# Keys by token in the last stage: a transposing DMA of 16-bit halves in place of TensorE transposes

## The chip, the cores and the metric

The kernel runs on one core of a Trainium2 chip. The core has five engines that each take their own instructions in the order in which the program was built: TensorE (PE in the profile, with its weight loads shown apart as PEld), VectorE (DVE), ScalarE (ACT), GpSimd (POOL) and SyncE (SP, which here only issues DMAs). They meet through semaphores, through SBUF (the on-chip memory), and through PSUM, eight banks of 128 partitions by 512 float32 in which matmuls leave their results. The metric is the device time of one execution in microseconds; the time of a kernel is the median of several runs. One more execution is profiled.

## The reference

The input is x, 8 sequences of 512 tokens with 512 features, float32. The output is x + s * silu(f). Both s and f come from the layer-normed tokens: s is linear attention over each sequence, f a mixture of 16 experts, of which each token takes 4, plus a gated shared expert. The part that the change touches is the attention, with 16 heads of 32 features, in 4 chunks of 128 tokens:

```python
q = (x @ Wq).reshape(b, n, HEADS, HEAD_DIM)
k = (x @ Wk).reshape(b, n, HEADS, HEAD_DIM)
v = (x @ Wv).reshape(b, n, HEADS, HEAD_DIM)
q = _lrpe_rotate(jax.nn.silu(q))
k = _lrpe_rotate(jax.nn.silu(k))
def step(S, qkv):
    qi, ki, vi = qkv
    scores = jnp.einsum('bthd,bshd->bhts', qi, ki) * D[None]
    o_intra = jnp.einsum('bhts,bshd->bthd', scores, vi)
    o_inter = jnp.einsum('bthd,bhde->bthe', qi * decay_q[None, :, :, None], S)
    S_new = lam_C[None, :, None, None] * S + jnp.einsum('bshd,bshe->bhde', ki * decay_k[None, :, :, None], vi)
    return (S_new, o_intra + o_inter)
```

(The two silus are written inside the rotation here; the reference has them on lines of their own.) The result o is gated, normalised by head and multiplied by Wo. The keys are thus needed in two layouts: features on partitions for the scores (qi with ki), and tokens on partitions for the state (ki, decayed, with vi). The state after the last of the four chunks is never used, so three chunks, 384 tokens, are enough for the second layout.

## The kernel before, in words

The kernel has three stages. The first (to about 330 us of the profiled execution) normalises all tokens, computes the routing and the shared expert, and attends over sequences 0 and 1. The second (about 330 to 752) runs 138 expert blocks of 128 gathered tokens; it fetches transposed tokens by a DMA that transposes 16-bit halves (L1019, issued on SP), which ScalarE joins into float32 (L1034). The last stage (752 to the end) attends over sequences 2 to 7 and, between these pieces, gathers and adds up each token's four expert results.

In the last stage `enter(FIRST)` starts sequence 2, `sequence(b, ...)` runs over b = 2 to 6 and `last_sequence` over 7. Each works on four groups g of four heads, that is 128 features. For a group `key` and `query` call `rotated` (L598 to L614): eight matmul instructions into a bank (L602), a silu on ScalarE (L607, tiles sk and sq), a shuffle and three products or sums on VectorE (L609 to L613), which leave kT and qT, features on partitions. `by_token` (L622) makes the second layout of the keys: three TensorE transposes (L629) into the bank pk, and a decaying product on VectorE (L632, tile kd). `scores` (L638) has the state matmuls of kd with v (L647) into the last 96 columns of the same bank pk, the score matmuls (L658) into four banks, and on VectorE the states (L661, L663), the decayed queries qd (L668) and the masked scores sc (L674). `output` (L679) multiplies qd by the state (L686) and sc by v (L692) into one bank, po, and gates it (L696). After the four groups come squares and the norm, and `project` (L735) with Wo, which for b < 7 is spread over the groups of the following sequence.

The PSUM banks go by tags: four "a" (scores, norm), one "k" (pk), one "m" (the key projection) and two "d", which the query projection pq, the projection pw and the output po take in turn. A bank is written again only when its last reader is done. Thus po of group 0 takes the bank of pq of group 2, and waits for the silu sq of group 2 on ScalarE; po of group 1 waits likewise for sq of group 3.

In `sequence`, group g's loop turn runs: scores(g), key(g + 2), by_token(g + 1), a projection, query(g + 2), another projection, output(g). So keys and queries are made two groups ahead. Between such steps, generators of the mixture (`mixture`, L1133) and its end (`last`, L1170) place their instructions: gathers (L1146) and additions (L1152, L1155) on GpSimd, sums on VectorE (L1157, L1160), a silu on ScalarE (L1163), the product with the attention (L1174), the addition of x on GpSimd (L1178) and the store on SP (L1179). The order on every engine is fixed when the program is built.

Of the kernel before, what the change touches and what calls it, by code (L numbers as in the profile page):

```python
# [10 lines left out]
F32 = mybir.dt.float32  # L11
# [3 lines left out]
U16 = mybir.dt.uint16  # L15
# [4 lines left out]
P = 128  # L20
# [75 lines left out]
def tile_block(ctx: ExitStack, tc: tile.TileContext, a: dict, out: bass.AP):  # L96
# [107 lines left out]
    @contextmanager  # L204
    def on_pe():

        with tc.issue_after(last_pe[-1]) if last_pe else nullcontext():
            yield
        traced = nc.cur_bb.bb.instructions
        last_pe.append(next(  # L210
            i for i in reversed(traced) if i.engine == mybir.EngineType.PE))
# [337 lines left out]

    between = [lambda: None]  # L550

    kept = []

    def value(b, t):
        if t == 0:
# [60 lines left out]
    def key(b, g):  # L616
        kT_of[g] = rotated(b, g, "k", wk)
# [4 lines left out]
    def by_token(b, g):  # L622

        if not kept:
            kept.append(bank("k", f"pk_{b}_{g}"))
        pk = kept[0]
        with on_pe():
            for c in range(NC - 1):
                nc.tensor.transpose(  # L629
                    pk[:, c * P : (c + 1) * P], kT_of[g][:, c * C : (c + 1) * C], ident)  # L630
        kd = scr[0].tile([P, NC - 1, HG, HD], F32, tag="kd", name=f"kd_{b}_{g}")
        nc.vector.tensor_tensor(  # L632
            kd, pk[:, : (NC - 1) * P].rearrange("p (c h d) -> p c h d", c=NC - 1, d=HD),
            dk[:, g * HG : (g + 1) * HG].unsqueeze(1).unsqueeze(3).to_broadcast(
                [P, NC - 1, HG, HD]), ALU.mult)
        kd_of[g] = pk[:, (NC - 1) * P :], kd

    def scores(b, g):  # L638

        pkv, kd = kd_of.pop(g)
        with on_pe():
            for c in range(NC - 1):
                for j in range(HG):
                    h = g * HG + j
                    nc.tensor.matmul(  # L647
                        pkv[j * HD : (j + 1) * HD, c * HD : (c + 1) * HD], lhsT=kd[:, c, j, :],
                        rhs=v_of[b][:, c, h * HD : (h + 1) * HD], start=True, stop=True)
        kT, qT = kT_of.pop(g), qT_of.pop(g)  # L650
        sc_of[g] = []
        pss = [bank("a", f"ps_{b}_{g}_{j}") for j in range(HG)]
        with on_pe():
            for c in range(NC):
                cs = slice(c * C, (c + 1) * C)
                for j in range(HG):
                    hs = slice(j * HD, (j + 1) * HD)
                    nc.tensor.matmul(  # L658
                        pss[j][:, cs], lhsT=kT[hs, cs], rhs=qT[hs, cs], start=True, stop=True)
        st = scr[0].tile([P, NC - 1, HD], F32, tag="state", name=f"state_{b}_{g}")  # L660
        nc.vector.tensor_copy(st[:, 0], pkv[:, :HD])  # L661
        for c in range(1, NC - 1):
            nc.vector.scalar_tensor_tensor(  # L663
                st[:, c], st[:, c - 1], lamc[:, g : g + 1], pkv[:, c * HD : (c + 1) * HD],
                ALU.mult, ALU.add)
        st_of[g] = st
        qd = scr[0].tile([P, NC - 1, C], F32, tag="qd", name=f"qd_{b}_{g}")
        nc.vector.tensor_tensor(  # L668
            qd, qT[:, C:].rearrange("p (c t) -> p c t", t=C),
            dq[:, g].unsqueeze(1).to_broadcast([P, NC - 1, C]), ALU.mult)  # L670
        qd_of[g] = qd
        for j in range(HG):
            s = scr[0].tile([P, NC, C], F32, tag="sc", name=f"sc_{b}_{g}_{j}", bufs=4)
            nc.vector.tensor_tensor(  # L674
                s, pss[j].rearrange("p (c t) -> p c t", t=C),
                dmask[:, g * HG + j].unsqueeze(1).to_broadcast([P, NC, C]), ALU.mult)
            sc_of[g].append(s)

    def output(b, g):  # L679
        po = bank("d", f"po_{b}_{g}")  # L680
        st, qd, sc = st_of.pop(g), qd_of.pop(g), sc_of.pop(g)
        with on_pe():
            for c in range(1, NC):
                for j in range(HG):
                    hs = slice(j * HD, (j + 1) * HD)
                    nc.tensor.matmul(  # L686
                        po[hs, c * C : (c + 1) * C], lhsT=st[hs, c - 1, :], rhs=qd[hs, c - 1, :],
                        start=(c == 1), stop=False)
            for c in range(NC):
                for j in range(HG):  # L690
                    h = g * HG + j
                    nc.tensor.matmul(  # L692
                        po[j * HD : (j + 1) * HD, c * C : (c + 1) * C],
                        lhsT=v_of[b][:, c, h * HD : (h + 1) * HD],
                        rhs=sc[j][:, c], start=False, stop=(c == NC - 1))
        nc.vector.tensor_tensor(on_of[b][:, g, :], po, on_of[b][:, g, :], ALU.mult)  # L696
# [43 lines left out]
    def enter(b, step=lambda: None):  # L740

        key(b, 0)
        step()
        query(b, 0)
        step()
        key(b, 1)
        step()
        by_token(b, 0)
        query(b, 1)
        step()  # L750

    def sequence(b, step, projected, before=None, defer=False, also=lambda: None):


        n = b + 1

        def project_tiles(q, ts):
            if q is not None:
                for t in ts:
                    projected(q, t, project(q, t))  # L760


        fill = ([0], [1], [2], [3], [], [], [], [])
        for g in range(G):
            scores(b, g)
            step()
            if g + 2 < G:
                key(b, g + 2)
            else:
                value(n, 2 * (g - 2))  # L770
            if g == 0 and b not in on_of:
                gate_3(b)
            if g + 1 < G:
                by_token(b, g + 1)
            project_tiles(before, fill[2 * g])
            step()
            if g + 2 < G:
                query(b, g + 2)
                if g + 3 == G and n not in xT_of:
                    load_xT(n)  # L780
            elif defer:
                (gate_1, gate_2)[g - 2](n)
            if g + 2 == G:
                value(n, 1)
            project_tiles(before, fill[2 * g + 1])
            if fill[2 * g + 1] == [NC - 1]:
                on_of.pop(before, None)
            output(b, g)
            step()
        v_of.pop(b)  # L790
        if n == FIRST:
            gate_1(n)
            squares(b)
            inverse(b)
            value(n, 3)
            normed(b)
            gate_2(n)
            return
        if defer:
            gate_3(n)  # L800
        value(n, 3)
        also()
        squares(b)
        step()
        inverse(b)
        key(n, 0)
        also()
        query(n, 0)
        normed(b)
        also()  # L810
        step()
        key(n, 1)
        by_token(n, 0)
        query(n, 1)
        also()
        if not defer:
            for gate, half in ((gate_1, [0, 1]), (gate_2, [2, 3])):
                gate(n)
                project_tiles(b, half)
                also()  # L820
            on_of.pop(b)
        step()

    def last_sequence(b, step, projected, before):
# [18 lines left out]
        def normed_of(g):  # L843
            rs = rs_of.pop(g)
            pbs = [bank(tag, f"pb_{b}_{g}_{c}")
                   for c, tag in enumerate("mddk" if g + 1 == G else "aaaa")]
            with on_pe():
                for c in range(NC):
                    cq = slice(c * Q, c * Q + H)
                    nc.tensor.matmul(  # L850
                        pbs[c][:, :C], lhsT=wge[cq, g * P : (g + 1) * P], rhs=rs[cq, :],
                        start=True, stop=True)
            for c in range(NC):
                oc = on_of[b][:, g, c * C : (c + 1) * C]
                nc.vector.tensor_tensor(oc, oc, pbs[c][:, :C], ALU.mult)
# [13 lines left out]
        for g in range(G):  # L869
            scores(b, g)  # L870
            step()
            if g + 2 < G:
                key(b, g + 2)
            if g > 1:
                project_before(2 * g - 3)
            if g:
                squares_of(g - 1)
            if g + 1 < G:
                by_token(b, g + 1)
            step()  # L880
            if g + 2 < G:
                query(b, g + 2)
            if g in (1, 2):
                project_before(2 * g - 2)
                normed_of(g - 1)
            output(b, g)
            step()
        kept.clear()
# [397 lines left out]
```

## Time and profile before

The median of 3 runs is 1228.07 us (1228.03 to 1228.19). The profiled execution:

| what | value |
|---|---|
| its own time | 1229.93 us |
| its span | 1228.1 us |
| mean granted TensorE clock | 0.989 |
| PE busy | 1170.0 us, 95% |
| DVE busy | 754.3 us, 61% |
| POOL busy | 441.8 us, 36% |
| ACT busy | 401.5 us, 33% |
| DMA, mean over the span | 177 GB/s |
| L629 transposes, all 96 | 16.2 us, 277 ns each |
| L1034 joins of the second stage, 138 | 105.8 us, 766 ns each |

Busy time is the time in which an engine executes; waiting on semaphores and issuing DMAs is not counted. The matmuls are pipelined, so the mean of one transpose is longer than the room that it takes between others. The span is from the first to the last instruction seen; the own time is the device's time of that same execution. A row of the timeline gives a start, a length, the engine, the line, the operation with its tiles (out<-in) and shapes, and in brackets how long the engine had been idle and what released it.

### The profile page before, as it was taken

What the parts mean: (1) busy time and instruction counts of PE and PEld (TensorE: products, weight loads), DVE (VectorE), ACT (ScalarE), POOL (GpSimd) and SP (SyncE); (2) the same over time, 40 slices, a digit from 0 to 9 for tenths busy, and PEclk for the clock granted to TensorE, in tenths of its full rate; (3) what the DMA queues carried; (4) which work ended last, traced back from release to release, by engine and by line L of the source; (5) the groups of instructions that cost most, each with busy time, mean ns of one, the idle gap of its engine ahead of it and who ended that gap; (6) DMA issues with size and microseconds to landing.
All of it is one profiled execution on the core that took longest, in us unless ns stands there. A gap on an engine that the chain in (4) does not pass through costs nothing. (4 is left out here: it accounts for less than half of the span.)

```text
span 1228.1 us, 21368 instructions
## 1 busy us (share of the span) xinstructions
PE 1170.0 (95%) x7734; PEld 690.8 (56%) x7734; DVE 754.3 (61%) x1638; ACT 401.5 (33%) x767; POOL 441.8 (36%) x426
## 2 busy tenths in 40 slices
PE   6998999989989999999999999999999999999997
PEld 3444554446467777777777775545545444445453
DVE  6378554899324444444444445849879589598784
ACT  3342333320264444444443441041140221411420
POOL 3222101100213333333333332833867827848211
PEclk9998999989999999999999999999999899999999
DMA  9784331182459999999998997822746626535011
GB/s 322 259 289 161 117 137 70 26 323 82 169 142 225 231 229 224 230 228 225 224 228 223 232 225 231 288 61 77 259 112 215 183 67 226 169 104 149 24 36 69
DMA packets 164599, 217.76 MB, mean 177 GB/s; under 512 B 90896, under 2 KB 99856, under 8 KB 162576
## 3 DMA queue, kind: packets, MB, share of 16 engines
q1 hardware_dynamic: 143216, 145.52, 39.9%
q0 software_dynamic: 21280, 70.88, 20.8%
q8 instruction: 64, 1.05, 0.4%
q14 instruction: 39, 0.32, 0.1%
HBM read 125.89 MB, written 72.35 MB: 161 GB/s over the span
## 5 line engine op out<-in xcount | busy, mean ns | idle before, releaser
L1051 PE MATMUL pgu<-wexp,xt 128*128 x1104 | 261.4, 380 | 0.8 <-ACT xt L1032 0.8
L1051 PEld LDWEIGHTS pgu<-wexp,xt 128*128 128x128 f32 x1104 | 209.0, 190 | 88.5 <-issue 42.8
L1010 POOL DMA_INDIRECT xg<-xn_d,slot x80 | 75.9, 949 | 248.5 <-DVE y L1081 162.5
L1056 DVE TENSOR_TENSOR slb<-slb,pgu 128x128 f32<-128x128 f32 x138 | 39.6, 287 | 196.4 <-ACT slb L1055 129.9
L1146 POOL DMA_INDIRECT yg<-y_d,posi x128 | 141.1, 1102 | 46.9 <-SPq L1113 19.3
L1034 ACT COPY xt<-pl 128x512 uint16<-128x512 uint16 x138 | 105.8, 766 | 140.2 <-DMA pl<-xg 86.8
L1072 PE MATMUL py<-wexp,hT 128*128 x276 | 141.3, 594 | 0.1
L560 PE MATMUL pv<-wv,xT 128*128 128x512 f32 x256 | 123.5, 622 | 5.2 <-DVE sh L372 4.1
L602 PE MATMUL pk<-xT,wk 128*128 128x512 f32 x256 | 120.5, 611 | 1.7 <-DVEq L1113 1.7
L602 PE MATMUL pq<-xT,wq 128*128 128x512 f32 x256 | 115.9, 593 | 0.0
L1178 POOL TENSOR_TENSOR xo<-xo,m 128x512 f32<-128x512 f32 x30 | 43.4, 1446 | 167.5 <-DVE m L1174 158.5
L735 PE MATMUL pw<-wo,on 128*128 128x512 f32 x224 | 100.8, 595 | 2.5 <-ACT so L908 1.8
L1010 POOL DMA_INDIRECT more<-xn_d,slot x58 | 54.8, 944 | 111.4 <-DVE y L1081 110.5
L560 PEld LDWEIGHTS pv<-wv,xT 128*128 128x128 f32 x256 | 47.4, 197 | 63.6 <-issue 55.6
L674 DVE TENSOR_TENSOR sc<-ps,dmask 128x512 f32<-128x512 f32 x128 | 79.4, 682 | 1.0 <-PE ps L658 1.0
L1081 DVE TENSOR_SCALAR y<-py,xg 128x512 f32<-128x512 f32 x80 | 60.0, 751 | 29.2 <-PE py L1072 28.8
L602 PEld LDWEIGHTS pq<-xT,wq 128*128 128x128 f32 x256 | 47.3, 191 | 52.2 <-issue 50.9
L602 PEld LDWEIGHTS pk<-xT,wk 128*128 128x128 f32 x256 | 46.4, 192 | 51.1 <-issue 48.6
L735 PEld LDWEIGHTS pw<-wo,on 128*128 128x128 f32 x224 | 41.3, 190 | 52.1 <-issue 44.7
L1055 ACT ACTIVATE slb<-pgu 128x128 f32<-128x128 f32 x138 | 38.3, 278 | 93.3 <-PE pgu L1051 88.9
L607 ACT ACTIVATE sk<-pk 128x512 f32<-128x512 f32 x32 | 19.1, 596 | 124.2 <-PE pk L602 102.4
L564 ACT COPY v<-pv 128x512 f32<-128x512 f32 x32 | 18.8, 588 | 122.2 <-PE pv L560 118.3
(168 smaller groups left out, 1766.7 us busy)
## 6 DMA issues: line engine op xcount, KB each, us to landing
y_d<-y SPq DMA_DIRECT2D x138, 256.0 KB
wexp<-in_experts SPq DMA_DIRECT2D x16, 768.0 KB
sh_d<-sh SPq DMA_DIRECT2D x32, 256.0 KB
m<-sh_d SPq DMA_DIRECT2D x32, 256.0 KB
xo<-in_x SPq DMA_DIRECT2D x32, 256.0 KB
out<-xo SPq DMA_DIRECT2D x32, 256.0 KB
x<-in_x SPq DMA_DIRECT2D x7, 1024.0 KB
xT_d<-xT SPq DMA_DIRECT2D x7, 1024.0 KB
```

The lines of the kernel that those rows point to most:

```text
L560: nc.tensor.matmul(pv, lhsT=xT_of[b][:, k, t * P : (t + 1) * P], rhs=wv[:, k, :], start=(k == 0), stop=(k == KC - 1))
L602: nc.tensor.matmul(ps, lhsT=w[:, k, g * P : (g + 1) * P], rhs=xT_of[b][:, k, :], start=(k == 0), stop=(k == KC - 1))
L674: nc.vector.tensor_tensor(s, pss[j].rearrange("p (c t) -> p c t", t=C), dmask[:, g * HG + j].unsqueeze(1).to_broadcast([P, NC, C]), ALU.mult)
L735: nc.tensor.matmul(pw, lhsT=on_of[b][:, g, t * P : (t + 1) * P], rhs=wo[:, g, :], start=(g == 0), stop=(g == G - 1))
L1010: nc.gpsimd.indirect_dma_start(out=row(i), out_offset=None, in_=xn_d, in_offset=bass.IndirectOffsetOnAxis(ap=slot[:, i : i + 1], axis=0))
L1034: nc.scalar.copy(xt[:, KP:, :].bitcast(U16).rearrange("p k (t h) -> p h k t", h=2), turned(i).rearrange("p (h k) t -> p h k t", h=2))
L1051: nc.tensor.matmul(pg[:, : 2 * F], lhsT=xt[:, k, :], rhs=wflat[:, bass.ds(off + k * 2 * F, 2 * F)], start=(k == 0), stop=(k == KC - 1))
L1056: nc.vector.tensor_tensor(sl, sl, pg[:, F : 2 * F], ALU.mult)
L1072: nc.tensor.matmul(py, lhsT=hT_of.pop(i), rhs=wflat[:, bass.ds(off_of.pop(i) + KC * 2 * F, D)], start=True, stop=True)
L1081: gone.append(nc.vector.tensor_scalar(y, py, row(i).bitcast(F32)[:, bass.ds(at, 1)], None, ALU.mult).ins)
L1146: nc.gpsimd.indirect_dma_start(out=yg, out_offset=None, in_=y_d, in_offset=bass.IndirectOffsetOnAxis(ap=posi[:, r, g : g + 1], axis=0))
L1178: nc.gpsimd.tensor_tensor(xo, xo, m, ALU.add)
```

## The change

For sequences 2 to 7 `by_token` no longer transposes on TensorE. GpSimd copies the 384 tokens of kT, seen as 16-bit numbers, so that low and high halves lie apart (tile kh, 128x768, one buffer). SP issues one transposing DMA of kh into kl (six blocks of 128x128 halves, two buffers). A new function `joined` has ScalarE write the halves side by side again into kt (float32 128x384, one buffer), and `decay`, the product on VectorE that was the end of `by_token`, is called at the start of `scores`. `by_token(b, 0)` moves ahead of `key(b, 1)`, both in `enter` and in the handover from one sequence to the next; `joined` stands ahead of `query(1)` for group 0, and ahead of `output(g)` for group g + 1. Sequences 0 and 1 keep the transposes. The state matmuls still write the last columns of the bank pk.

```diff
--- before.py
+++ after.py
@@ -549,7 +549,7 @@
 
     between = [lambda: None]
 
-    kept = []
+    kept, kl_of, kt_of = [], {}, {}
 
     def value(b, t):
         if t == 0:
@@ -624,21 +624,46 @@
         if not kept:
             kept.append(bank("k", f"pk_{b}_{g}"))
         pk = kept[0]
-        with on_pe():
-            for c in range(NC - 1):
-                nc.tensor.transpose(
-                    pk[:, c * P : (c + 1) * P], kT_of[g][:, c * C : (c + 1) * C], ident)
+        if b < FIRST:
+            with on_pe():
+                for c in range(NC - 1):
+                    nc.tensor.transpose(
+                        pk[:, c * P : (c + 1) * P], kT_of[g][:, c * C : (c + 1) * C], ident)
+            kt = pk[:, : (NC - 1) * P]
+        else:
+
+            kh = scr[0].tile([P, 2, (NC - 1) * C], U16, tag="kh", name=f"kh_{b}_{g}")
+            nc.gpsimd.tensor_copy(
+                kh, kT_of[g][:, : (NC - 1) * C].bitcast(U16).rearrange("p (t h) -> p h t", h=2))
+            kl = scr[0].tile([P, 2 * (NC - 1), P], U16, tag="kl", name=f"kl_{b}_{g}", bufs=2)
+            nc.sync.dma_start_transpose(kl, kh.rearrange("p h t -> p (h t)"))
+            kl_of[g] = kl
+            return
+        decay(b, g, kt)
+
+    def joined(b, g):
+        if g in kl_of:
+            kt = scr[0].tile([P, (NC - 1) * P], F32, tag="kt", name=f"kt_{b}_{g}")
+            nc.scalar.copy(
+                kt.bitcast(U16).rearrange("p (c n h) -> p h c n", c=NC - 1, h=2),
+                kl_of.pop(g).rearrange("p (h c) n -> p h c n", h=2))
+            kt_of[g] = kt
+
+    def decay(b, g, kt):
         kd = scr[0].tile([P, NC - 1, HG, HD], F32, tag="kd", name=f"kd_{b}_{g}")
         nc.vector.tensor_tensor(
-            kd, pk[:, : (NC - 1) * P].rearrange("p (c h d) -> p c h d", c=NC - 1, d=HD),
+            kd, kt.rearrange("p (c h d) -> p c h d", c=NC - 1, d=HD),
             dk[:, g * HG : (g + 1) * HG].unsqueeze(1).unsqueeze(3).to_broadcast(
                 [P, NC - 1, HG, HD]), ALU.mult)
-        kd_of[g] = pk[:, (NC - 1) * P :], kd
+        kd_of[g] = kept[0][:, (NC - 1) * P :], kd
 
     def scores(b, g):
 
 
 
+        joined(b, g)
+        if g in kt_of:
+            decay(b, g, kt_of.pop(g))
         pkv, kd = kd_of.pop(g)
         with on_pe():
             for c in range(NC - 1):
@@ -743,9 +768,13 @@
         step()
         query(b, 0)
         step()
+        if b >= FIRST:
+            by_token(b, 0)
         key(b, 1)
         step()
-        by_token(b, 0)
+        if b < FIRST:
+            by_token(b, 0)
+        joined(b, 0)
         query(b, 1)
         step()
 
@@ -785,6 +814,7 @@
             project_tiles(before, fill[2 * g + 1])
             if fill[2 * g + 1] == [NC - 1]:
                 on_of.pop(before, None)
+            joined(b, g + 1)
             output(b, g)
             step()
         v_of.pop(b)
@@ -808,9 +838,13 @@
         query(n, 0)
         normed(b)
         also()
+        if n >= FIRST:
+            by_token(n, 0)
         step()
         key(n, 1)
-        by_token(n, 0)
+        if n < FIRST:
+            by_token(n, 0)
+        joined(n, 0)
         query(n, 1)
         also()
         if not defer:
@@ -883,6 +917,7 @@
             if g in (1, 2):
                 project_before(2 * g - 2)
                 normed_of(g - 1)
+            joined(b, g + 1)
             output(b, g)
             step()
         kept.clear()
```

## The prediction

> **What bounds the kernel now.** I read the busy times first, then the last stage cut by sequence, then the timeline of one sequence, then the rows of the operations that the change borrows. By busy time the matmuls fill the span:
>
> ```profile
> PE 1170.0 (95%) x7734; PEld 690.8 (56%) x7734; DVE 754.3 (61%) x1638; ACT 401.5 (33%) x767; POOL 441.8 (36%) x426
> ```
>
> The stretches of sequences 3 to 6 (start and end, length, busy time of PE, weight loads, DVE, ACT and POOL, granted clock, DMA share, GB/s):
>
> ```profile
> 821.00:897.00 76.00, 75.45 (x666) 38.04 (x668) 61.59 (x105) 20.30 (x33) 41.83 (x35) 1.00 0.45 146
> 897.00:984.00 87.00, 82.71 (x678) 41.20 (x678) 65.03 (x104) 20.73 (x34) 64.56 (x56) 0.96 0.58 175
> 984.00:1065.00 81.00, 78.08 (x678) 38.67 (x670) 66.11 (x106) 20.64 (x34) 50.38 (x42) 1.00 0.47 148
> 1065.00:1144.00 79.00, 76.39 (x679) 38.21 (x671) 65.30 (x104) 20.59 (x34) 55.52 (x46) 1.00 0.45 131
> ```
>
> PE is idle 0.6 to 4.3 us of each, so PE is the bound, and DVE, at 65 of 80, is close behind. What hangs on what is in the timeline of sequence 5 (start, length, engine, line, operation):
>
> ```profile
> 1011.34 0.69 DVE L613 TENSOR_TENSOR kT<-kT,swk 128x512 f32<-128x512 f32 x1
> ...
> 1012.63 0.60 ACT L607 ACTIVATE sq<-pq 128x512 f32<-128x512 f32 x1 [6.57 <-PE pq L602]
> 1012.68 3.70 PE L735 MATMUL pw<-wo,on 128*128 128x512 f32 x8
> ...
> 1014.83 0.73 DVE L609 STREAM_SHUFFLE swq<-sq 128x512 f32<-128x512 f32 x1
> 1015.45 2.14 DVE L611 TENSOR_TENSOR qT<-sq,cos 128x512 f32<-128x512 f32 x1
> ...
> 1016.31 0.86 PE L686 MATMUL po<-qd,state 32*32 32x128 f32 x24
> ...
> 1030.46 0.69 DVE L613 TENSOR_TENSOR kT<-kT,swk 128x512 f32<-128x512 f32 x1
> ...
> 1035.44 0.86 PE L686 MATMUL po<-qd,state 32*32 32x128 f32 x24
> ```
>
> The output matmuls po of group 0 (1016.31) take the bank that pq of group 2 held, so they need sq_2, the silu that empties it on ACT. It is done at 1013.2: 3.1 us of room. po of group 1 (1035.44) needs sq_3, done at 1032.2: 3.3 of room. These two waits decide my forecast; the key's other reader, the state matmuls L647, has 10 to 24 us after kT in groups 1 to 3.
>
> What is removed, in one group:
>
> ```profile
> 1152.07 3.70 PE L602 MATMUL pk<-xT,wk 128*128 128x512 f32 x8
> 1155.61 0.49 PE L629 MATMUL pk<-ident,kT 128*128 128x128 f32 x3
> 1155.93 3.60 PE L602 MATMUL pq<-xT,wq 128*128 128x512 f32 x8
> ```
>
> Eight projections hold PE for 3.44 (the spacing of the rows at 1155.93 and, of the following one, 1159.46 is 3.53), so 1152.07 to 1155.93 leaves about 0.42 for the three transposes. What is added exists in the expert stage at two thirds of its size (issue on SP, join on ACT):
>
> ```profile
> 598.88 1.22 SPq L1019 DMA_TRANSPOSE pl<-more  x1
> ...
> 602.22 0.76 ACT L1034 COPY xt<-pl 128x512 uint16<-128x512 uint16 x1 [0.62 <-DMA pl<-more]
> ```
>
> From issue to the join 3.34 us, ACT waiting at its end for the DMA.
>
> **The Trainium skill.** [...] "DMA: Bandwidth & Descriptors", "Anatomy of one DMA — SWDGE (gpsimd) path", in a general note: DMA engines don't wait on semaphores, the issuing sequencer does before it dispatches; so a transposing DMA that waits on SP holds what follows it there. SP's waits for the additions before its stores show such waiting. "TensorE: Matmul & The Clock Gate", "Part 1: The HAM clock gate": after an idle window of a few us TensorE's clock falls to half. Here eight matmuls after 3.46 us of idle (start 30.04) took 5.40 against 3.70: agrees, +1.7. "GPSIMD Engine Reference", specifications: GpSimd and VectorE share their SBUF port. Here the product at 1015.45 took 2.14 instead of 0.68, beside a POOL addition.
>
> **The change, part by part.** In b = 2 to 7, four groups each:
>
> - Removed: 24 times three transposes, 24 x 0.42 = 10.1 us of PE, and the waits before them for the bank's last reader (DVE state L663), 2.1.
> - Added on POOL: 24 copies of 128x768 halves. The copy of halves L268, 128x512, takes 0.705 to 0.715; x1.5 = 1.07.
> - Added on SP: 24 transposing DMAs with 1.2 to 1.8 of issue. Data of 1.5 times the size: between the 3.3 of the row above and 5.5 if it queues behind the gathers and stores (DMA share 0.45 to 0.58); I take 4.1.
> - Added on ACT: 24 joins, 0.766 x 1.5 = 1.15 (0.766 is the mean of L1034). ACT has 60 us free of 80, so its time is nothing; its place is not. kd on DVE reads SBUF in place of a bank: 0.55 either way (0.3 to 0.7).
> - Moved: by_token ahead of the next key; kd of groups 2 and 3 goes to just after the state copy L661; DVE executes the same number. kd_1 keeps its place ahead of the shuffle of sk_2 and now waits for kt_1; behind it stand the key of group 2 and the mixture's products, and that wait is in the chain below through sk_2, which ends later still.
>
> Each join waits on ACT for its DMA. In the order of instructions as built, in sequences 3 to 6, kt_2 stands ahead of sq_2 and kt_3 ahead of sq_3; kt_1 stands ahead of sk_2 in all. So sq_2, ready before as soon as ACT was free, now waits for kT_2, then copy 1.15 (with its wait), transfer 4.1, join 1.2 and silu 0.7: 7.15 after kT_2. POOL and SP are in order too: kh_1 stands behind 7 to 9 gathers and additions issued since kh_0 (0.95 + 0.30 and 1.28 + 0.16 each), late by 0, 0.8, 2.7 and 3.6 in sequences 3 to 6. On SP each kl stands ahead of stores that wait long anyway (301.7 us of SP's waits are for L1178), so loads behind it lose nothing; kl_6_0 delays one store by about 7, with nothing behind it needed. On POOL kh_0 of sequence 6 holds the gathers about 9 us, inside the 11.6 that POOL idled there. Gathers at the start of sequence 2 start 14 later; POOL idled 35.7 at 848, so covered.
>
> Sequence 5 in full. kT_1 is there at 1001.0; kh_1 runs 1003.7 to 1004.8 behind POOL's gathers, lands 1008.9, kt_1 ends 1010.1, the mixture's silu and sk_2 follow to 1011.3 (before 1006.1), kT_2 at 1013.9 (before 1012.0). Plus 7.15: sq_2 ends 1021.1, po_0 starts 1021.2 instead of 1016.31: +4.9 of idle PE. The shuffle of sq_2 on DVE moves from 1014.83 to 1021.1, +6.3. From there DVE has no pause until kT_3 (1030.46 + 0.69 = 1031.15), so kT_3 comes at 1037.4; plus 7.15 sq_3 ends 1044.5, and po_1 starts 1044.6 instead of 1035.44: +9.2, less 0.42 for the last transposes: +8.8. The rest of the sequence is bound by PE with DVE waiting, and DVE's lag is made up there. The same for the others: po_1 from 869.51 to 876.6, +6.7 net; 948.14 to 957.5, +9.0; 1115.69 to 1125.2, +9.1.
>
> Sum: sequences 3 to 6, 6.7 + 9.0 + 8.8 + 9.1 = 33.6. Sequence 2 (the query silus stand ahead of the joins here, but kt_1 still ahead of sk_2, and transfers are slow in its start) +2.5, an estimate between 0 and 5. Sequence 7: kt_2 stands ahead of its first square, 2.9 - 0.8 = about +2. Transposes of group 0 in sequences 3 to 6, not counted yet: 4 x 0.33 = -1.3. Clock: eight stalls of 4 to 5 us, some of which cross the window, +1.7 at most each; I take +2.7 (0 to 13). Total +39.5. The profiled execution took 1229.93 (span 1228.1 and 1.8 around it) and becomes 1269.4; the median of the runs is 1228.07, 1.86 lower, so about 1267; I say 1266.
>
> A us of transfer counts three times in a sequence (kt_1 ahead of sk_2, then kt_2, then kt_3), 12 times in all: with 3.0 instead of 4.1 it is 1266 - 13, with 5.5 it is 1266 + 17; with the bounds of sequences 2 and 7 the likeliest's own range is 1250 to 1286.
>
> **Rivals.**
>
> A, the other side: the chain is hidden. For it: L647 needs kd 10 to 24 us after kT, PE sheds 10.1 + 2.1, and everything else is on engines with room. Then PE sets 1228 - 10 = 1218. The point from which it decides: po starts 4.3 us after kT at both gates (1012.03 to 1016.31, 1031.15 to 1035.44), silu 0.7 off leaves 3.6 from kT to the end of kt. Against it: copy and join alone are 2.35 of this, so the transfer would have to land in 1.3 us, where the expert stage's smaller one took 3.3. 0.05.
>
> B, milder: a short transfer (under 3 us) or only one gate per sequence, the lag being made up between po_0 and po_1 because PE's stall lets DVE and POOL run apart. Then +4 to 5 per sequence, 16 to 20 + 3 - 1 = +18 to 22: 1246 to 1250. For it: the 2.14 products beside POOL would shrink to 0.68. 0.14.
>
> C, worse: SP or POOL becomes the gate. If transfers queue behind the 256 KB stores and gathers (over 5.5), each gate grows by 2 or more and each stall brings the half clock: over 1290, about 1305. 0.09.
>
> **How the numbers follow.** Likeliest 0.72, A 0.05, B 0.14, C 0.09. Range 1242 to 1292: it holds the likeliest and B, and leaves out A and C. Less than 0.2% (2.5 us) can't be told from no change in this kernel; only A, or a part of it that just pays its way, ends there or below: faster 0.04, same 0.01, slower 0.95.
>
> **What would show it.** L629 with 24 instead of 96 transposes. Silu sq of L607 in sequences 3 to 6 waiting behind the joins, with ACT's idle time put down to the DMA of kl; PE idle before L686 of some 5 and 4 us at groups 0 and 1, near none at groups 2 and 3; the copy to join 5 to 6 us. Wrong if L686 shows no new idle (A), if the idle stands at L647 instead (kd as the gate), if sequences 2 or 7 lose as much as the others, or if expert blocks differ at all.

## The result, and the profile after

The changed kernel takes 1261.36 us, the median of 5 runs (1260.08 to 1267.52), beside 1228.03 for the kernel before in 5 runs: slower by 33 us, ratio 1.0300 with a 95% interval of 1.0279 to 1.0321. The forecast was 1266 in 1242 to 1292. The profiled execution is the longest of the five (1267.52, span 1265.7), so its differences sum to 37.6 where the medians differ by 33.

The page of the kernel after, first its busy times:

```profile
PE 1176.3 (93%) x7662; PEld 688.9 (54%) x7662; DVE 760.9 (60%) x1638; ACT 423.8 (33%) x791; POOL 462.0 (36%) x450
```

PE has 72 instructions fewer and is busy 6 us longer. That is the first thing that the forecast had not foreseen. All of it lies in the last stage. That stage as a whole in the kernel before and after, in the view of stretches (start and end, length, busy PE, weight loads, DVE, ACT, POOL, granted clock, DMA share, GB/s):

```profile
752.99:1228.10 475.11, 452.45 (x3970) 228.07 (x3970) 362.65 (x623) 113.58 (x181) 266.18 (x222) 0.99 0.45 141
```

```profile
751.12:1265.70 514.58, 459.70 (x3898) 226.80 (x3898) 369.11 (x623) 135.86 (x205) 285.95 (x246) 0.96 0.48 139
```

Stage one and two together are 1.9 us shorter, the last stage is 39.5 longer. PE's idle time in it goes from 22.7 (475.1 - 452.5) to 54.9, +32.2. Its busy time goes up by 7.3, although the transposes removed there were 12.1 us of busy time: the rest of PE's work, unchanged, took 19 us longer. The granted clock goes with it, 0.99 before and 0.96 after: by this ratio alone the 440.3 us of that work (452.45 - 12.1) would take 14 us longer, an estimate from the two rows. The other 5 are not accounted for.

The same view of sequences 3 to 6 of the kernel after, cut where the same instructions stand:

```profile
822.50:908.70 86.20, 76.79 (x655) 37.94 (x652) 66.71 (x105) 23.90 (x38) 56.99 (x49) 0.98 0.51 156
908.70:1002.70 94.00, 85.52 (x667) 42.41 (x668) 62.18 (x104) 24.86 (x39) 61.43 (x53) 0.91 0.55 160
1002.70:1089.60 86.90, 77.01 (x642) 37.39 (x640) 67.47 (x106) 23.09 (x36) 57.31 (x50) 0.98 0.54 153
1089.60:1176.80 87.20, 78.95 (x683) 38.17 (x675) 64.55 (x104) 25.32 (x40) 58.74 (x50) 0.98 0.47 133
```

They were 76, 87, 81 and 79 long; each is 6 to 10 longer. PE was idle 0.6 to 4.3 us in each, and is now idle 8 to 10. VectorE is about as busy as before (260.9 in the four, 258.0 before).

What PE waited for in the last stage (engine, tile and line, then what it waited for: us in all, times, longest):

```profile
PE pw L760 <- DVE m L1209: 12.3, 5, 4.4
PE pk L672 <- DVE kd L654: 12.2, 4, 4.8
PE po L711 <- ACT sq L607: 9.4, 6, 2.2
```

Before, the waits for m and for kd were 0.6 and 1.3, and there was none for the silu sq. Only the third is the wait that the forecast was built on. Another 7.6 us are waits for VectorE's masked scores sc, of which the kernel before shows none. VectorE's own waits for sq show the forecast's gate more plainly, before and after:

```profile
DVE swq L609 <- ACT sq L607: 8.4, 10, 1.7
```

```profile
DVE swq L609 <- ACT sq L607: 39.1, 15, 5.1
```

The timeline of sequence 5 shows two of the three waits of PE, and the chain from the key to the query's silu:

```profile
1033.92 0.69 DVE L613 TENSOR_TENSOR kT<-kT,swk 128x512 f32<-128x512 f32 x1
1034.53 0.68 DVE L1209 TENSOR_TENSOR m<-m,pw 128x512 f32<-128x512 f32 x1
1034.73 0.82 POOL L636 COPY kh<-kT 128x768 uint16<-128x768 uint16 x1 [3.69 <-issue]
...
1035.26 5.40 PE L760 MATMUL pw<-wo,on 128*128 128x512 f32 x8 [4.43 <-DVE m L1209]
...
1035.58 1.22 SPq L639 DMA_TRANSPOSE kl<-kh  x1
...
1038.43 1.06 ACT L647 COPY kt<-kl 128x768 uint16<-128x768 uint16 x1
...
1039.36 0.58 ACT L607 ACTIVATE sq<-pq 128x512 f32<-128x512 f32 x1
...
1040.59 0.86 PE L711 MATMUL po<-qd,state 32*32 32x128 f32 x24
...
1055.33 3.70 PE L760 MATMUL pw<-wo,on 128*128 128x512 f32 x8 [1.09 <-DVE m L1209]
...
1059.53 1.04 ACT L647 COPY kt<-kl 128x768 uint16<-128x768 uint16 x1 [6.74 <-DMA kl<-kh]
...
1060.45 0.58 ACT L607 ACTIVATE sq<-pq 128x512 f32<-128x512 f32 x1
...
1061.09 0.86 PE L711 MATMUL po<-qd,state 32*32 32x128 f32 x24 [2.05 <-ACT sq L607]
```

Read it from the top. The second projection pw of group 0 needs a bank whose reader is VectorE's product m (1034.53), and on VectorE that product stands behind the key of group 2 (1033.92). PE waits 4.43 us for it. The eight matmuls after that wait take 5.40; those after a wait of 1.09, at 1055.33, take 3.70. Meanwhile kT_2 goes its way: copy, transposing DMA, join, and only then sq_2, which was ready long before. It ends at 1039.94, just before pw does, so here po waits for nobody. In group 1 it does, for 2.05.

The join itself, in the page's list of groups (busy, mean ns, then the idle time before it and what ended it):

```profile
L647 ACT COPY kt<-kl 128x768 uint16<-128x768 uint16 x24 | 25.3, 1054 | 133.6 <-DMA kl<-kh 133.6
```

ScalarE stood still 133.6 us at the head of its queue for these transfers.

### The profile page after: what moved, and what is told of

It reads as the page before. It is cut to its first block, busy times and chain, and to the rows that moved or that the text cites. A ratio compares the mean times of both kernels' runs of the same rounds, so it can differ in the third digit from the quotient of the medians.

```text
span 1265.7 us, 21356 instructions
## 1 busy us (share of the span) xinstructions
PE 1176.3 (93%) x7662; PEld 688.9 (54%) x7662; DVE 760.9 (60%) x1638; ACT 423.8 (33%) x791; POOL 462.0 (36%) x450
## 3 DMA queue, kind: packets, MB, share of 16 engines
q8 instruction: 64, 1.05, 0.4%
## 5 line engine op out<-in xcount | busy, mean ns | idle before, releaser
L602 PE MATMUL pk<-xT,wk 128*128 128x512 f32 x256 | 124.5, 628 | 1.7 <-DVEq L1148 1.7
L760 PE MATMUL pw<-wo,on 128*128 128x512 f32 x224 | 106.1, 621 | 14.1 <-DVE m L1209 12.3
L602 PE MATMUL pq<-xT,wq 128*128 128x512 f32 x256 | 118.6, 604 | 0.0
L1045 POOL DMA_INDIRECT more<-xn_d,slot x58 | 54.9, 947 | 110.1 <-DVE y L1116 109.2
L636 POOL COPY kh<-kT 128x768 uint16<-128x768 uint16 x24 | 19.7, 823 | 141.1 <-DVE kT L613 92.4
L647 ACT COPY kt<-kl 128x768 uint16<-128x768 uint16 x24 | 25.3, 1054 | 133.6 <-DMA kl<-kh 133.6
```

What stands on the lines that cost most here:

```text
L602: nc.tensor.matmul(ps, lhsT=w[:, k, g * P : (g + 1) * P], rhs=xT_of[b][:, k, :], start=(k == 0), stop=(k == KC - 1))
L760: nc.tensor.matmul(pw, lhsT=on_of[b][:, g, t * P : (t + 1) * P], rhs=wo[:, g, :], start=(g == 0), stop=(g == G - 1))
L1045: nc.gpsimd.indirect_dma_start(out=row(i), out_offset=None, in_=xn_d, in_offset=bass.IndirectOffsetOnAxis(ap=slot[:, i : i + 1], axis=0))
```

## The experiments

Two theories stood at the start. ACT: joins that wait for their DMA hold the silus behind them. WORK: the copies, transfers and joins cost as such. In the cuts of code below, `behind(ACT)` gives an instruction its place on ScalarE right behind the one that the program text has before it. Each ratio is to the kernel before on the same chip; its median was 1216.59, 1225.97 and 1216.16 in the three groups of runs (e1 to e4, e5 to e8, e9 to e12), so times are compared within a group only.

**The joins behind the silus (e1).**

```diff
-            nc.scalar.copy(kt..., kl...)
+            with behind(ACT):
+                nc.scalar.copy(kt..., kl...)
```

> The changed kernel, but each join takes its place on ScalarE behind the instruction that the program text has before it: kt_1 to kt_3 behind the query silus sq_2 and sq_3 instead of ahead of them, kt_0 behind sk_1. Theory ACT (joins that wait for their DMA hold the silus behind them): PE's waits for the product m (12.3 us), for sq (9.4) and most of the cold clock go; the wait for kd of group 0 (12.2) stays: 1235, between 1226 and 1245. Rival WORK (the copies on GpSimd and the transposing DMAs cost as such, by the port shared with VectorE and by DMA time): the order of the joins changes little, 1252 or more.

Measured: 1261.59, ratio 1.0382 (1.0350 to 1.0413). Theory ACT expected 7 us over the kernel before (1235 beside 1228); it was 45, and WORK's number, 24 or more, came true. Yet the waits that ACT named went: for sq none is left, for m 1.5. In their place PE's waits read

```profile
PE pk L673 <- DVE kd L655: 44.6, 16, 6.5
```

and the timeline at group 0 of sequence 5:

```profile
1009.94 1.05 ACT L648 COPY kt<-kl 128x768 uint16<-128x768 uint16 x1
...
1014.05 0.72 DVE L609 STREAM_SHUFFLE swk<-sk 128x512 f32<-128x512 f32 x1
...
1016.87 0.55 DVE L655 TENSOR_TENSOR kd<-kt,dk 128x384 f32<-128x384 f32 x1
1017.47 0.55 PE L673 MATMUL pk<-v,kd 128*32 128x32 f32 x24 [4.64 <-DVE kd L655]
```

The join ended at 1011.0, and VectorE came to the decay product kd 5.9 us later: it now stands behind the shuffle and two products of the key of group 1 in VectorE's order, where in the changed kernel it stood ahead of them. A later join came with a later place for its reader. Moving the wait off one queue moved it to another.

**The chain alone (e2).**

```diff
         kd_of[g] = pk[:, (NC - 1) * P :], kd      # transposes kept
+        if b >= FIRST:
+            kh = ...; nc.gpsimd.tensor_copy(kh, halves of kT)
+            kl = ...; nc.sync.dma_start_transpose(kl, kh)   # nobody reads kl
```

> The kernel before with its transposes, and beside them the copy kh on GpSimd and the transposing DMA kl, which nobody reads; no join. Every other instruction keeps its order. Theory ACT: 1228 to 1232, since nothing on ScalarE waits for the DMA. Rival WORK: 1245 to 1260.

Measured: 1220.86, ratio 1.0041 (1.0022 to 1.0060), 4 to 5 us, at the top of ACT's 0 to 4 and far from WORK's 17 to 32. The work on GpSimd, SP and the DMA queues is about a seventh of the loss. WORK in its plain form is out.

**The chain and a join that nobody reads (e3).**

```diff
+            joined(b, g + 1)      # kt written on ScalarE, read by nobody
             output(b, g)
```

> The one above, and the join kt on ScalarE too, which nobody reads; in sequences 3 to 6 the joins stand ahead of sq as in the changed kernel. The decay product still takes the transposes' bank. Theory ACT: the loss comes with the join: 1250 to 1262 (the changed kernel's 33, less 12 of waits for kd, plus up to 10 of transposes that it keeps). Rival WORK: no more than 5 above the one without the join. A second rival, KD (PE waits for the late decay product, which is fed by the join): about as without the join, for nobody waits for kt here.

Measured: 1241.54, ratio 1.0210 (1.0183 to 1.0237). One instruction of 1.05 us per group on an engine that is idle two thirds of the time costs 21 us over e2, with its output thrown away. PE's and ScalarE's waits:

```profile
PE po L700 <- ACT sq L607: 8.2, 7, 2.3
```

```profile
ACT kt L648 <- DMA kl<-kh: 123.8, 23, 9.6
```

This is the wait of the forecast with little beside it (kd 3.8, in e2 2.1); VectorE waits 32.4 for sq, in e2 10.0. kd doesn't depend on the join here, which rules out KD as the cause of these 21 us. Over the kernel before it is 25 us, inside the 22 to 34 that theory ACT expected.

**The same join behind the silus (e6).**

```diff
-            nc.scalar.copy(kt..., kl...)
+            with behind(ACT):
+                nc.scalar.copy(kt..., kl...)
```

> The run with transposes, chain and unread join, with one edit: each join stands behind the query silus on ScalarE instead of ahead of them. Theory ACT: the loss of 2.1% falls to that of the chain without a join, 0.2 to 0.7% over the kernel before. Rival JOIN-WORK (1.05 us of join each, its reads and writes, cost as such): 1.7% or more stays.

Measured: 1237.71, ratio 1.0094 (1.0067 to 1.0120). VectorE's waits for sq are back at 11.2, with 4.3 more in one stop that is put down to a join. With e3, the place of the join is 1.2% (about 14 us); besides the joins six other instructions moved on ScalarE, and none on VectorE or GpSimd. Theory JOIN-WORK, with 1.7% or more, is out, but ACT's 0.2 to 0.7% was too little as well: 0.5% stays over e2. The two intervals just don't meet, and no row of PE's waits accounts for it (those of the transposes for VectorE's state are 10.4 here and 10.0 in e2).

**No transposes, nothing added (e4), and one transpose for three (e5).** e4 leaves all 72 out, e5 leaves 48 out and uses one chunk three times. Both compute other states.

```diff
-            for c in range(NC - 1):                            # before
+            for c in range(NC - 1 if b < FIRST else 0):        # e4, kd reads kT
+            for c in range(NC - 1 if b < FIRST else 1):        # e5
                 nc.tensor.transpose(...)
```

> The kernel before without its 72 transposes in sequences 2 to 7 and with nothing in their place: the decay product reads the keys as they are, not transposed, so the states are others. What removing them from PE is worth at most. Theory PE (PE is the bound, 0.42 a group and 2.1 of waits): 1216 to 1219. Rival DVE (VectorE is what sets the pace once PE is relieved): 1224 to 1228.

> The kernel before with one transpose in place of three in each group of sequences 2 to 7 (the decay product reads that chunk three times, so the states are others). The order on VectorE stays as it was but for one product, unlike in the run without any transpose, where products moved. Theory PE-ROOM (PE is the bound and each transpose left out is time won, 48 x 0.14 = 6.7 us): 5 to 7 us below the kernel before. Theory DVE-PACE (VectorE's order sets when PE goes on; PE only waits where it worked, and its clock falls in the waits): within 2 us of the kernel before.

Measured: e4 1226.55, ratio 1.0089 (1.0062 to 1.0115), slower, which neither of its theories had; e5 1227.27, ratio 0.9998 (0.9983 to 1.0013). What PE sheds is worth nothing. In e4 kd also reads SBUF in place of a bank and moved on VectorE, ahead of the masked scores and of m, and PE waits there:

```profile
PE pg L573 <- DVE sc L674: 9.9, 3, 6.2
PE pw L735 <- DVE m L1174: 9.2, 4, 3.3
```

e5 keeps VectorE's order but for one product, and shows the worth by itself. DVE-PACE said so; PE-ROOM expected 5 to 7 us.

**The decay product early (e7).**

```diff
-            kt_of[g] = kt             # decayed at the start of scores
+            decay(b, g, kt)           # right behind the join in the text
```

> The changed kernel with the joins behind the query silus as in the first run, and the decay product placed in the program text right behind its join instead of at the start of the scores, so that it stands some ten products earlier on VectorE. Theory TWO GATES (the loss has two causes that take turns: a join ahead of a silus on ScalarE, or a decay product far back on VectorE): PE's 44.6 us of waits for kd fall under 12, 0.4 to 1.2% over the kernel before. Rival LATENCY (kT to kt is too long in any order): PE waits for kd 25 us or more, 2.5% or more over it.

Measured: 1265.43, ratio 1.0300 (1.0271 to 1.0330), PE's waits for kd 41.7. Theory TWO GATES expected 0.4 to 1.2%. But the run hardly tests it: as built, the product stands two or three places earlier in two groups of sequence 2 and one of sequence 7, and nowhere else, so the run is nearly e1 again, and doesn't support LATENCY either. The place in the order followed the join, not the text.

**Group 0 on TensorE (e11).** The other groups stay as in e7; `by_token` of group 0 goes back behind the next key, as in the kernel before (that part is not shown).

```diff
-        if b < FIRST:
+        if b < FIRST or g == 0:
             ... nc.tensor.transpose
```

> The kernel with joins behind the silus and the decay right behind its join, but with group 0 of every sequence by TensorE transposes as before, the other three groups by the DMA. In the run without this PE waited 41.7 us for kd, 24.6 of it in group 0. Theory TWO GATES: PE's waits for kd fall to some 17 us, 1.0 to 1.8% over the kernel before in place of 3.0. Rival: the waits move on to the later groups, 2.5% or more stays.

Measured: 1236.20, ratio 1.0164 (1.0134 to 1.0194), PE's waits for kd 23.5. A little under half of the loss of e7 goes with group 0, whose state matmuls follow soonest after `by_token`. That is within TWO GATES' 1.0 to 1.8%, but the waits did not fall to 17 as it expected: 2.0 of them are still in group 0, and those of the other groups grew by 4.4.

**Nothing of VectorE behind the join (e8, e12).** e8 decays kT ahead of the split, with a table in that layout, and the state matmuls read the join's output. e12 puts the decay on ScalarE right behind the join. Both have the joins behind the silus.

```diff
+            ke = kT * dkt                          # e8, VectorE, ahead of kh
-            nc.vector.tensor_tensor(kd, kt, dk)    # e12
+            for j in range(HG):
+                nc.scalar.activation(kd[:, :, j, :], kt of head j, AF.Copy, scale=dk[:, j])
```

> The changed kernel with the joins behind the query silus, and the decay applied ahead of the split, to kT with a table in its layout, so that the state matmuls read the join's output and VectorE has nothing between join and PE. Theory TWO GATES: 0 to 1% over the kernel before, a wait for kt at group 0 of 1 to 3 us per sequence. Rival LATENCY: 2.5% or more.

> The changed kernel with joins behind the query silus and the decay product also on ScalarE, right behind its join, so that VectorE's in-order queue no longer stands between the join and the state matmuls. Theory IN-ORDER (the loss is places in two queues, not the length of the chain): PE's waits for kd fall under 12 us, between 0.5% below and 0.8% over the kernel before. Rival LATENCY: 2% or more over it.

Measured: e8 1252.78, ratio 1.0214 (1.0188 to 1.0240), between its two theories (1% at most, 2.5% or more); e12 1239.62, ratio 1.0180 (1.0155 to 1.0206). Both theories missed e12: IN-ORDER, right on the waits for kd, by a per cent, and LATENCY, which asked for 2% or more, by so little that the interval reaches it. So LATENCY is not out. PE's waits in e12:

```profile
PE pw L766 <- DVE m L1215: 16.0, 5, 4.3
PE pk L678 <- ACT kd L664: 7.1, 8, 4.5
```

The wait for kd is nearly gone, 4.5 of its 7.1 in one stop at the start of sequence 2. PE comes up against m instead, once in each of sequences 3 to 6, 3.2 to 4.3 us at a time, with VectorE working without a pause up to there. With kd off its queue, VectorE is still the one that PE meets in the first groups of a sequence. In e8 it is the same: 16.0 for m.

**VectorE relieved in the kernel before (e9), and then fewer transposes (e10).** e10 leaves 48 transposes out as e5 does.

```diff
-        nc.vector.tensor_tensor(kd, pk, dk, ALU.mult)
+        for j in range(HG):
+            nc.scalar.activation(kd[:, :, j, :], pk of head j, AF.Copy, scale=dk[:, j])
```

> The kernel before, transposes and all, with the decay product of sequences 2 to 7 on ScalarE instead of VectorE (four scaled copies from the bank, one per head). VectorE loses its 24 products of 0.55 us, 13.1 in sum, and nothing else moves on it, on PE or on GpSimd. Theory DVE-PACE: with VectorE relieved the stops of PE and the cold clock after them shrink: 3 to 10 us below the kernel before. Rival PE-ONLY (VectorE's room was enough): within 2 us of it.

> The one above with one transpose in place of three in each group (the decay takes that chunk three times, so the states are others). Theory DVE-PACE: once VectorE is relieved, room on PE is worth something, so that the same 48 transposes that were worth nothing (ratio 0.9998) bring 3 to 7 us against the one above. Rival COLD (what matters is only whether PE stops for anybody): no difference, within 2 us.

Measured: e9 1212.31, ratio 0.9960 (0.9941 to 0.9980); e10 1209.30, ratio 0.9935 (0.9914 to 0.9956). e9 computes everything and is faster than the kernel before: 13 us less on VectorE brought 4, within DVE-PACE's 3 to 10. No other instruction changed its place on PE, VectorE or GpSimd. The 48 transposes that were worth nothing in e5 seem to be worth 3 us here, the low end of what was expected, but the intervals of e9 and e10 overlap, so this last step is only likely.

## Why the prediction was right, and where it was not

It was right in sign and size, by a mechanism that is a good part of the loss and not all of it; that the sum came within 5 us of the median is in part luck, as the terms show.

**The gate on ScalarE.** Right: joins ahead of the silus hold them, and e3 against e6 shows what that costs. Too large: the forecast gave 33.6 us to sq_2 and sq_3 holding po. The waits for sq are 9.4, and the order of the joins is worth about 14 in e3 and e6. The failing step is "po_0 starts 1021.2 instead of 1016.31: +4.9 of idle PE". The idle time at that point is there, 4.43 in sequence 5, but it stands one matmul group earlier, before pw, and is ended by VectorE's m. The kernel before could have told. The product that pw waits for there is

```profile
1011.95 0.68 DVE L1174 TENSOR_TENSOR m<-m,pw 128x512 f32<-128x512 f32 x1
```

It ended at 1012.63, and pw started at 1012.68: there was no room, while the silu had 3.1. The first of the three places in which a us of transfer was to count, kt_1 ahead of sk_2, was no gate: in sequences 3 to 6 VectorE came to the shuffle of sk_2 1.8 to 3.1 us after that silu had ended.

**kd.** "L647 has 10 to 24 us after kT in groups 1 to 3" was right, and left group 0 out, where kT's transposes and L647 were only 4 us apart. All four waits for kd (12.2) are in group 0 of sequences 2, 3, 5 and 6. The prediction had named idle time at these matmuls as a sign against itself; it came, beside the idle time at po. "0.55 either way" was wrong too. The product over all its 24 executions (shortest, median, longest in ns), before and after:

```profile
L632 DVE TENSOR_TENSOR kd<-pk,dk x24: 542/551/559, 763.9 to 1191.0; 128x384 f32<-128x384 f32 x24
```

```profile
L654 DVE TENSOR_TENSOR kd<-kt,dk x24: 541/546/2035, 769.3 to 1225.3; 128x384 f32<-128x384 f32 x24
```

Read from SBUF, it took 0.93 to 2.04 in the four cases that met one of GpSimd's additions; read from the bank, 0.55 to 0.56 in all six. In e1 eight met one and in e11 twelve (0.71 to 2.32, 14 us in sum over 0.55 each), so that a part of the waits for kd there may be this and not the place in the order. No run separates the two.

**The transposes.** The list of parts has 10.1 us of PE and 2.1 of waits as removed; the sum took 3.8 of it (0.42 in each of sequences 3 to 6, 1.3 for their groups 0, 0.8 in sequence 7). e5, which leaves out two thirds of the transposes in the kernel before, measured nothing (-2.1 to +1.6). Where the room went isn't settled: in e5's profile, taken on another chip, PE's idle time in the last stage is 21.6 against 22.7, so the stops did not grow, and its other work took 3 us longer at a granted clock of 0.98 against 0.99.

**The clock.** This term was too small. +2.7, with 13 as its bound, was allowed; PE's unchanged work took 19 us longer, an estimated 14 of it by the granted clock, which was 0.91 in sequence 4. A long stop costs its length and then the slow matmuls after it: 5.40 in place of 3.70 after the 4.43.

**The chain.** GpSimd's copy took 0.82 and not 1.07, the transfer from the copy's end to the join's start 2.8 to 5.0 (9.2 and 6.6 in sequence 2), median 3.1 against 4.1, the join 1.05 against 1.15. From the end of kT to the end of sq it was 5.3 and 6.4 in the two timeline cases, against 7.15. kh_1 was to be late by up to 3.6 behind the gathers; all 24 copies began about 0.1 us after their key.

**By sequence**, from po of group 3 to the next, sequences 2 to 7 lost 3.2, 10.3, 7.0, 5.9, 8.2 and 5.2; forecast were 2.5, 6.7, 9.0, 8.8, 9.1 and 2, before the clock and group 0's transposes. (In sequence 4 the kernel before had lost time itself: its eight pv matmuls at 968.02 took 6.22.) In sequences 3 to 6 most of it, 5.4 to 6.2, is there by po of group 0, and group 1 adds 0.9 to 2.4, where the forecast for sequence 5 had 4.9 and 3.9. Sequence 7's 5.2 is nearly sequence 5's 5.9, another sign that the prediction had named against itself: PE stood 3.44 us there before the first square's sums (1210.65), for VectorE's masked scores, and the eight projections after it took 6.33. That the rest of a sequence makes up VectorE's lag was right: from group 2 to 3 po loses 1.4 at most and gains up to 1.2. Errors of both signs made the sum look better than its parts: too much for ScalarE and the transfer, too little for kd, m and the clock.

**The rivals.** A, all hidden, was wrong twice: e3 shows that the chain isn't hidden, and e5 found no gain in fewer transposes. B's cause, a stop that lets VectorE run faster beside GpSimd, wasn't there: 43 products met an addition and a gather, at 1.55 us on average, where before 48 did at 1.55. C's transfers of over 5.5 occurred twice, both in sequence 2, and not as the rule.

**What stays open.** Taken as steps, the ratios are: chain 0.4%, join as work 0.5%, its place 1.2%, and 0.9% as what remains of the 3.0, with the kd that now depends on the join and the transposes gone. No run takes this last step by itself, and what in the unread join costs 0.5% out of the way isn't known. They were not all taken on one chip, and e12 shows that mending two of the causes brings 1.2 points, not the sum. Why VectorE's work from the norm to m is late against PE in e12, with less to do, isn't settled; that PE runs ahead of it is what the trace shows. In e2, e3 and e6, which keep the transposes, PE stops 10 to 11 us before them, for VectorE's state (2.1 in the kernel before); in the kernel after, e8 and e12, which have none, it stops 12 to 16 before pw, for m. So PE meets VectorE in all of these, in another place; that the transposes were a gate which only moved is not shown.

## What to carry to other kernels

A cheap instruction that waits for a long transfer costs what stands behind it in its engine's queue; look at the built order of that queue, not at the engine's busy share. Before taking work off the busiest engine, find who ends its waits: here 48 transposes on a PE at 95% were worth nothing, and 13 us off VectorE were worth 4. And when a stall is moved off one queue, look where the built order then puts what depended on it.

## What the runs showed of the hardware that was not expected

Of VectorE's 128x512 products and sums that stand alone in the timeline of the last stage of the kernel after, the 60 that ran beside a gather alone took 0.68 us, as the 114 with GpSimd idle; the 12 beside the copy of halves alone took 0.74, the 20 that met an addition alone 0.90, and the 43 that met an addition and a gather 1.55 on average (a longer product also meets more). So it is GpSimd's two-input additions that go with a longer VectorE, hardly its copies and not its gathers. "GPSIMD Engine Reference" of the Trainium skill, specifications, names VectorE instructions of two SBUF inputs among those that contend with GpSimd. The decay product agrees: beside an addition it took 0.55 from PSUM in six of six cases, and 0.93 to 2.04 from SBUF. Over its 24 executions that made 4 us more of VectorE (17.5 in sum, 13.2 before).
